# Sorting tokens by pair of experts: from marks at the end to lists in DRAM, written sequence by sequence

## The chip, the cores and the metric

The kernel runs on one core of a Trainium2 chip. The metric is the device time of one execution in microseconds (us); lower is better. Times are medians over runs; the profile is of one execution, taken by the hardware profiler. Engines are named as in the profile: PE (TensorE matmul), PEld (TensorE weight load), DVE (VectorE), ACT (ScalarE), POOL (GpSimd), SP (SyncE, which issues most DMAs). A name with a q, as SPq, is that engine's queue.

## The reference

One transformer block on 16 sequences of 512 tokens, 256 wide, in fp32. A layernorm feeds two branches, and both are added to the input:

```python
xn = layernorm(x)
q, k, v = xn @ Wq + bq, xn @ Wk + bk, xn @ Wv + bv      # 16 heads of 16
q, k = elu(q) + 1, elu(k) + 1
kv = einsum('bkhd,bkhm->bhdm', k, v)                    # linear attention
out = einsum('bqhd,bhdm->bqhm', q, kv) / max(einsum('bqhd,bkhd->bqh', q, k), eps)
attention = out @ Wo + bo
shared = swiglu(xn @ w_in.T) @ w_out.T
h = swiglu(xn @ w1.T)                                   # 512 wide, one for all experts
routed = sum(h * w_se[:, e] @ w2[e].T for e in range(8))
result = x + attention + shared + routed
```

The routing `w_se` picks for each token one of two groups of four experts, and the best two experts of that group. So a token belongs to one of 12 pairs of experts (6 to a group).

## The kernel before

There are 8192 tokens, in 64 tiles of 128 (`TT`; four to a sequence, `NT`). The work has two stages. In the first, a loop over the 16 sequences `b` computes attention, the shared branch and `h`, routes each token, and writes for each token a row of 770 numbers to DRAM (`h_d`): `h`, everything but the routed part, and the two weights of its pair. In the second, the tokens are taken sorted by pair, in tiles of 128 of one pair, at least 67 (`SURE`) and at most 75 (`TILES`). For each tile the rows are gathered with an indirect DMA (`Tiles.rows`, L943), turned (`turn`, L964 to L976), multiplied with the two experts' weights (`sums`, L993), weighted and added (L1000, L1003), and scattered to the output rows (L1006). To know which token stands where, the second stage needs two tables of [128 rows, 75 tiles]: `source` (the token to read) and `goal` (the row to write; too large for a place that stays empty, so that nothing is written). Making these two tables is what the change is about.

In iteration `b` of the loop come: the front of sequence b+1 (`residual` on POOL, L390; `project`, L412 to L430; `route`), `summarize` (L689), the normalization of b+2, the rows of `h` (`hidden_rows`, 14 products of 512 columns, L595), the key sum of b+1 (`key_sum`: two adds on POOL, L676 and L677, one product with ones, L679, and a copy `ksb` on DVE, L681), `attend` for b+1, the shared branch (`hidden`, L621), the small products with Wv and Wo (`values`, L708; `mix`, L731), and the outputs (`outputs`, L768; the add L777). The first sequence has plainer forms of the two branches (`first_rows`, L644 and L651; `first_hidden`, L663 and L669; weights are differenced beside them, L527). For the last sequence alone, the products with Wv and Wo are called from inside `hidden`.

`route` leaves in `hot` (bf16, [128, 64, 12]) a one at each token's pair, and POOL adds up in `ahead_of` (L515) how many tokens of each pair the earlier tiles had in the same partition.

The order on each engine comes from a scheduler that works at build time, except where the code fixes it: `keep_in_program_order` pins steps to the written order, `high_priority` moves steps ahead, `issue_after` holds one behind another. [...] Buffers come from pools that rotate: `ps_mm` has six PSUM banks, `ps_y` two, `work` two of each tag. A tile that takes a buffer waits for the last reader of the tile that had it. The key sums and the outputs take `ps_y` (the outputs of sequence 14 take `ps_mm`).

The sorting is `order()` (L806 to L924), a generator: each `yield` gives control back, and the loop calls `next` at chosen places, in part through `between`. Its steps: counts of each pair by two fp32 products (L813, L815); starts of the pairs, rounded up to whole tiles (L829); the slot of each of the 8192 tokens (L833 to L847); and the marks. A mark turns the slots round: for each of eight groups of eight tiles, DVE writes which of 128 rows (L877) and which of 75 tiles (L882) a token goes to, multiplied by the token's number (L886, L890), and PE adds `lo` times `hi` over all 64 tiles into one PSUM tile `pi` (L894, 64 bf16 products of 150 columns). From `pi` come `source` and `goal` (L908 to L923). These steps lie in the last two iterations: counts and slots in iteration 14, the marks between the outputs of 14 and the products of `hidden_rows` of 15.

Of the kernel before, what the change touches and what calls it, by code (L numbers as in the profile page):

```python
# [10 lines left out]
FP = mybir.dt.float32  # L11
AF = mybir.ActivationFunctionType
ALU = mybir.AluOpType
# [8 lines left out]
def block_kernel(  # L22
# [55 lines left out]
    TG = 8  # L78
    TR = 5
    assert TT % TG == 0  # L80
# [10 lines left out]

    h_d = dram.tile([TT * P, ROW], FP, name="h_d")

# [101 lines left out]
    def load_expert(i):  # L195
# [21 lines left out]
    before = const.tile([P, P], FP)  # L217
    nc.gpsimd.affine_select(
        out=before, in_=ones, pattern=[[1, P]],
# [4 lines left out]
    for j in range(EG):  # L224
        nc.gpsimd.memset(place[:, :, j : j + 1], float(j))
    BF = mybir.dt.bfloat16
    count = const.tile([P, P], BF)
    nc.gpsimd.iota(count, pattern=[[1, P]], base=0, channel_multiplier=0,
                   allow_small_or_imprecise_dtypes=True)
    number = const.tile([P, TT], BF)  # L230
    nc.gpsimd.iota(number, pattern=[[1, TT]], base=1, channel_multiplier=0,
                   allow_small_or_imprecise_dtypes=True)
    row = const.tile([P, 1], FP)
    nc.gpsimd.iota(row, pattern=[[0, 1]], base=0, channel_multiplier=1,
# [282 lines left out]
    def between(b, n):  # L517

        if b + 2 >= B:
            for _ in range(n or 0):  # L520
                next(steps_of_order)
# [68 lines left out]
    def hidden_rows(b, xs7, then):  # L590

        rows = {}

        def product(to, u, i, start, stop):
            tc.keep_in_program_order(nc.tensor.matmul(  # L595
                to, lhsT=xs7[i][:, ts(u, P)], rhs=w1_in[W7[i]], start=start, stop=stop,
                skip_group_check=True,
            ))

        def room(u, half):  # L600
            rows[u, half] = work.tile([P, HID], FP, tag="hr", name=f"hr_{b}_{u}_{half}", bufs=4)
            return rows[u, half]

        def done(u, half, silu, product):
            nc.sync.dma_start(out=h_d[ts(b * NT + 2 * half + u, P), 0:HID], in_=rows[u, half])

        seven(f"phr_{b}", product, lambda a: a, room, done, lambda n: between(b, then(n)))
# [89 lines left out]
    def small_sums(b, shape, name):  # L697

        if b + 1 == B:
            return ps_y.tile(shape, FP, tag="py", name=f"{name}_{b}"), tc.keep_in_program_order  # L700
        return ps_mm.tile(shape, FP, tag="mm", name=f"{name}_{b}"), lambda step: step
# [25 lines left out]
    def mix(b, vk):  # L727

        pm, pin = small_sums(b, [P, KD, D], "pm")
        for c in range(KD):  # L730
            pin(nc.tensor.matmul(  # L731
                pm[:, c, :], lhsT=vk[:, c, :], rhs=wo_sb[:, c, :], start=True, stop=True
            ))
        kvo = one.tile([P, KD, D], FP, tag="kvo", name=f"kvo_{b}")
        with tc.high_priority() if b + 1 == B else nullcontext():
            nc.scalar.copy(kvo, pm)
        return kvo
# [21 lines left out]
    def outputs(b, t, qT, kvo, hs):  # L759
# [6 lines left out]
        parts += [(qT[:, c, ts(t, P)], kvo[:, c, :]) for c in range(KD)]  # L766
        for i, (a, w) in enumerate(parts):
            nc.tensor.matmul(po, lhsT=a, rhs=w, start=(i == 0), stop=(i == len(parts) - 1))  # L768
        return po

    def gather(b, res, qT, kvo, hs, placed, then):

        for t in range(NT):
# [5 lines left out]
            between(b, then(t))  # L779
# [26 lines left out]
    def order():  # L806

        I32, U32 = mybir.dt.int32, mybir.dt.uint32
        total = keep.tile([P, NP], FP)
        nc.vector.tensor_copy(total, ahead_of[:, TT, :])  # L810
        pc = ps_mm.tile([P, 2 * NP], FP, tag="mm", name="pc")
        tc.keep_in_program_order(
            nc.tensor.matmul(pc[:, 0:NP], lhsT=before, rhs=total, start=True, stop=True)  # L813
        )
        nc.tensor.matmul(pc[:, NP:], lhsT=ones, rhs=total, start=True, stop=True)  # L815
        pcs = keep.tile([P, 2 * NP], FP)
# [3 lines left out]
        nc.vector.tensor_scalar(ci, pcs[:, NP:], float(P - 1), None, ALU.add)  # L820
# [5 lines left out]
        nc.vector.tensor_copy(runs[0][:, PAD:], ci)  # L826
        for i, d in enumerate((1, 2, 4, 8)):
            a, r = runs[i % 2], runs[(i + 1) % 2]
            nc.vector.tensor_tensor(r[:, PAD:], a[:, PAD:], a[:, PAD - d : PAD - d + NP], ALU.add)  # L829
        starts = runs[0][:, PAD - 1 : PAD - 1 + NP]  # L830

        off = keep.tile([P, NP], FP)
        nc.vector.tensor_tensor(off, pcs[:, 0:NP], starts, ALU.add)  # L833
        sl = one.tile([P, TT, NP], FP, tag="low", name="sl")
        nc.vector.tensor_tensor(
            sl, ahead_of[:, 0:TT, :], off.unsqueeze(1).to_broadcast([P, TT, NP]), ALU.add
        )
        nc.vector.tensor_tensor(sl, sl, hot, ALU.mult)
        slot = keep.tile([P, TT], I32)
        slf = keep.tile([P, TT], FP)  # L840
        nc.vector.tensor_reduce(slf, sl, AX.X, ALU.add)
        nc.vector.tensor_copy(slot, slf)
        part = keep.tile([P, 2, TT], I32)
        nc.vector.tensor_scalar(part[:, 0, :], slot, P - 1, None, ALU.bitwise_and)
        nc.vector.tensor_scalar(part[:, 1, :], slot, 7, None, ALU.arith_shift_right)
        place_of = keep.tile([P, 2, TT], BF)
        nc.vector.tensor_copy(place_of, part)  # L847
# [12 lines left out]
        nc.vector.tensor_copy(where, of)  # L860
        yield


        pi = ps_y.tile([P, 2 * TILES], FP, tag="py", name="pi")

        los = x_all.rearrange("p b t d -> p (b t d)").bitcast(BF).rearrange("p (n t j) -> p n t j", t=TG, j=P)
        his = [
            a[:, B % 2].rearrange("p t d -> p (t d)").bitcast(BF)[:, 0 : TG * 2 * TILES].rearrange(
                "p (t i n) -> p t i n", t=TG, i=2
            )  # L870
            for a in (qq_all, kk_all, xn_all)
        ]

        def marks(g):
            row_of, tile_of = (place_of[:, i, ts(g, TG)].unsqueeze(2) for i in range(2))
            lo, hi = los[:, g % 4], his[g % 3]
            nc.vector.tensor_tensor(  # L877
                lo, count.unsqueeze(1).to_broadcast([P, TG, P]), row_of.to_broadcast([P, TG, P]),
                ALU.is_equal,
            )  # L880
            at_tile = one.tile([P, TG, TILES], BF, tag="at_tile", name=f"at_tile_{g}")
            nc.vector.tensor_tensor(  # L882
                at_tile, count[:, 0:TILES].unsqueeze(1).to_broadcast([P, TG, TILES]),
                tile_of.to_broadcast([P, TG, TILES]), ALU.is_equal,
            )
            nc.vector.tensor_tensor(  # L886
                hi[:, :, 0, :], at_tile,
                number[:, ts(g, TG)].unsqueeze(2).to_broadcast([P, TG, TILES]), ALU.mult,
            )
            nc.vector.tensor_scalar(hi[:, :, 1, :], at_tile, row, None, ALU.mult)  # L890

        def add(g):
            for t in range(TG):
                tc.keep_in_program_order(nc.tensor.matmul(  # L894
                    pi, lhsT=los[:, g % 4, t, :], rhs=his[g % 3][:, t].rearrange("p i n -> p (i n)"),
                    start=(g + t == 0), stop=(g * TG + t == TT - 1),
                ))


        for g in range(TT // TG + 2):  # L900
            if g > 1:
                add(g - 2)
                yield
            if g < TT // TG:
                marks(g)
                yield
        pis = keep.tile([P, 2, TILES], FP)
        nc.vector.tensor_copy(pis.rearrange("p i n -> p (i n)"), pi)  # L908
        free = keep.tile([P, TILES], FP)
        nc.vector.tensor_scalar(free, pis[:, 0, :], 0.0, float(2 * TT * P), ALU.is_equal, ALU.mult)  # L910
        tok = keep.tile([P, TILES], FP)
        nc.vector.scalar_tensor_tensor(
            tok, pis[:, 0, :], float(P), pis[:, 1, :], ALU.mult, ALU.add
        )
# [6 lines left out]
        nc.vector.tensor_scalar(source, tok, float(-P), 0.0, ALU.add, ALU.max)  # L921
        goal = keep.tile([P, TILES], U32)
        nc.vector.scalar_tensor_tensor(goal, tok, float(-P), free, ALU.add, ALU.add)  # L923
# [109 lines left out]
    xs[2] = load_x(2)  # L1033
    for b in range(B):
# [4 lines left out]
        if b + 2 == B:  # L1039
# [4 lines left out]
            steps_of_order = order()  # L1044
        if b + 1 == B:
            sums7 = token_sums(b, xnT)
            hidden_rows(b, sums7, {2: 2, 6: 2, 9: 2, 13: 2}.get)
# [3 lines left out]
            *lists, filled = next(steps_of_order)  # L1051
# [9 lines left out]
        if b == 0:  # L1061
            first_rows(xnT)
        elif b + 1 < B:
            sums7 = token_sums(b, xnT)
            hidden_rows(b, sums7, {9: 1}.get)
# [5 lines left out]
        if b + 2 == B:  # L1071
            next(steps_of_order)
# [3 lines left out]
        if b + 1 < B:  # L1076
# [13 lines left out]
        if b + 2 == B:  # L1090
            next(steps_of_order)
# [5 lines left out]
        else:  # L1097
            gather(b, res, qT, kvo, hs, normed[b + 2][2]() if b + 2 < B else None, {0: 2, 1: 2, 3: 2}.get)
# [66 lines left out]
```

## Time and profile before

| | us |
|---|---|
| median of 3 runs (1039.69 to 1040.49) | 1040.03 |
| the profiled execution | 1033.23 |
| its span, first to last instruction | 1031.5 |
| PE busy | 1004.9 |
| DVE busy | 779.4 |
| ACT busy | 488.1 |
| POOL busy | 254.8 |

A row of the time line gives start, length, engine, line, operation, `output<-input` with the sizes, and how many instructions it holds; at its end in brackets the idle time of the engine before it and what ended that. A row of the waits says who waited for whom: time in all, number of times, longest. PE ran at full clock (1.00 in each stretch looked at). The fp32 products are recorded as two matmuls each. One sequence of the middle takes about 47 us (the first `project` product of the sequence at 644.7 and of the next at 692.07); the second stage begins at 789.84 us.

### The profile page before, as it was taken

How to read it: one execution, taken by the hardware profiler on the slowest of the kernel's cores; microseconds unless marked ns; L12 is line 12 of the kernel's file. 1: busy time of each engine (PE TensorE's matmuls, PEld its weight loads, DVE VectorE, ACT ScalarE, POOL GpSimd, SP SyncE). 2: the span in 40 equal slices, each digit the busy share in tenths (PEclk: the TensorE clock that was granted, in tenths of full speed). 3: DMA queues.
4: the chain of work that ended last, by engine and by line, in shares of the span. 5: the costliest groups of instructions: out<-in, count | busy, mean ns of one | idle time of the engine just before them, and what ended most of it. 6: DMA issues, size and time to landing. Idle time of an engine off the chain costs nothing. (4 is left out here: it accounts for less than half of the span.)

```text
span 1031.5 us, 12407 instructions
## 1 busy us (share of the span) xinstructions
PE 1004.9 (97%) x3704; PEld 681.7 (66%) x3704; DVE 779.4 (76%) x1974; ACT 488.1 (47%) x893; POOL 254.8 (25%) x359
## 2 busy tenths in 40 slices
PE   7999999999999999999999999999899999999996
PEld 5466868677786868686777768686667344444442
DVE  5978687878778787878787877868975776666663
ACT  3525353535445253535343534425136576766671
POOL 5302020111202021110202020201012766555652
PEclk9999999999999999999999999999999999999999
DMA  7063534525152522314141313221235755555440
GB/s 220 16 177 107 141 104 101 147 59 154 51 163 54 161 84 81 122 42 143 37 128 56 110 55 123 72 77 61 62 110 146 225 172 153 147 156 157 150 147 30
DMA packets 130339, 116.08 MB, mean 113 GB/s; under 512 B 72637, under 2 KB 114109, under 8 KB 130272
## 3 DMA queue, kind: packets, MB, share of 16 engines
q1 hardware_dynamic: 120064, 77.43, 25.7%
q0 software_dynamic: 9392, 37.58, 12.2%
q8 instruction: 31, 0.51, 0.2%
q10 hardware_dynamic: 816, 0.27, 0.2%
q14 instruction: 36, 0.29, 0.1%
HBM read 65.36 MB, written 50.27 MB: 112 GB/s over the span
## 5 line engine op out<-in xcount | busy, mean ns | idle before, releaser
L993 PE MATMUL py<-w_sb,hT 128*128 x536 | 230.7, 592 | 1.7 <-DVE hT L976 1.6
L993 PEld LDWEIGHTS py<-w_sb,hT 128*128 128x128 f32 x536 | 101.7, 190 | 130.1 <-issue 129.1
L768 PE MATMUL po<-wout_sb,hs_all 128*128 128x256 f32 x480 | 116.6, 380 | 1.4 <-DVE hs_all L580 1.4
L390 POOL TENSOR_TENSOR res<-x_all,bo_sb 128x256 f32<-128x256 f32 x64 | 48.5, 792 | 274.4 <-DMA h_d<-res 203.4
L768 PEld LDWEIGHTS po<-wout_sb,hs_all 128*128 128x128 f32 x480 | 89.2, 190 | 15.1 <-DVE hs_all L580 3.4
L1006 POOL DMA_INDIRECT out<-y,goal x67 | 67.8, 1012 | 76.3 <-DVE y L1003 65.3
L676 POOL TENSOR_TENSOR k<-kk_all 128x512 f32<-128x512 f32 x16 | 20.9, 1307 | 258.3 <-DVE sm L458 247.7
L777 DVE TENSOR_TENSOR res<-po,res 128x256 f32<-128x256 f32 x60 | 25.4, 424 | 76.6 <-PE po L768 76.5
L398 ACT ACTIVATE km<-km 128x1024 f32<-128x1024 f32 x16 | 16.9, 1057 | 138.7 <-DVE km L397 134.4
L595 PE MATMUL phr_w<-w_sb,ss 128*128 128x512 f32 x120 | 61.5, 594 | 2.2 <-DVE ss L538 1.9
L768 PE MATMUL po<-kvo,qT 128*128 128x256 f32 x240 | 61.7, 383 | 0.0
L621 PE MATMUL phs_w<-ss,win_sb 128*128 128x256 f32 x240 | 61.6, 379 | 0.0
L621 PE MATMUL phs_t<-xnT,win_sb 128*128 128x256 f32 x240 | 61.6, 379 | 0.0
L595 PE MATMUL phr_t<-w_sb,xnT 128*128 128x512 f32 x120 | 61.3, 593 | 0.0
L595 PE MATMUL phr_t<-w_sb,ss 128*128 128x512 f32 x120 | 59.4, 597 | 0.0
L621 PE MATMUL phs_t<-ss,win_sb 128*128 128x256 f32 x240 | 59.1, 379 | 0.0
L689 PE MATMUL pxk<-kk_all,xn_all 128*128 128x256 f32 x256 | 58.0, 379 | 0.0
L412 PE MATMUL pk<-wkr_sb,xnT 128*128 128x266 f32 x240 | 57.2, 387 | 0.0
L423 PE MATMUL pq<-w_sb,xnT 128*128 128x256 f32 x240 | 54.2, 379 | 0.0
L689 PEld LDWEIGHTS pxk<-kk_all,xn_all 128*128 128x128 f32 x256 | 48.5, 190 | 6.7 <-issue 0.2
L964 ACT COPY hb<-qq_all 32x256 f32<-32x256 f32 x108 | 43.4, 402 | 17.1 <-DMA qq_all<-h_d,source 9.7
L412 PEld LDWEIGHTS pk<-wkr_sb,xnT 128*128 128x128 f32 x240 | 45.4, 190 | 8.0
(216 smaller groups left out, 1966.0 us busy)
## 6 DMA issues: line engine op xcount, KB each, us to landing
h_d<-hr SPq DMA_DIRECT2D x64, 256.0 KB, 2.5
q_d<-qq_all SPq DMA_DIRECT2D x16, 512.0 KB, 2.8
qb<-q_d SPq DMA_DIRECT2D x64, 128.0 KB, 3.1
w_sb<-in_w SPq DMA_DIRECT2D x64, 128.0 KB, 3.5
h_d<-res SPq DMA_DIRECT2D x60, 129.0 KB, 1.9
x_all<-in_x SPq DMA_DIRECT2D x15, 512.0 KB, 4.8
xn_d<-xn_all SPq DMA_DIRECT2D x14, 512.0 KB, 3.9
xb<-xn_d SPq DMA_DIRECT2D x56, 128.0 KB, 2.8
```

The source lines that it names most:

```text
L390: nc.gpsimd.tensor_tensor(res[:, t, 0:D], xt[:, t, :], bo_sb, ALU.add)
L412: nc.tensor.matmul(pk, lhsT=xnT[:, k, ts(t, P)], rhs=wkr_sb[:, k, :], start=(k == 0), stop=(k == KD - 1),)
L423: nc.tensor.matmul(pq[:, t, :], lhsT=xnT[:, k, ts(t2 + t, P)], rhs=wq_sb[:, k, :], start=(k == 0), stop=(k == KD - 1),)
L595: tc.keep_in_program_order(nc.tensor.matmul(to, lhsT=xs7[i][:, ts(u, P)], rhs=w1_in[W7[i]], start=start, stop=stop, skip_group_check=True,))
L621: tc.keep_in_program_order(nc.tensor.matmul(split(to)[:, f, :], lhsT=win_in[W7[i]][:, ts(2 * u + f, P)], rhs=xs7[i], start=start and f == ...
L676: nc.gpsimd.tensor_tensor(k2, kk[:, 0:2, :], kk[:, 2:4, :], ALU.add)
L689: nc.tensor.matmul(pxk[:, c, :], lhsT=xn[:, t, ts(c, P)], rhs=kk[:, t, :], start=(t == 0), stop=(t == NT - 1),)
L768: nc.tensor.matmul(po, lhsT=a, rhs=w, start=(i == 0), stop=(i == len(parts) - 1))
L777: nc.vector.tensor_tensor(res[:, t, 0:D], po, res[:, t, 0:D], ALU.add)
L964: nc.scalar.copy(there[ts(q, Q), a - near, 0:n, :], self.hg[ts(a, Q), 0:n, ts(q, W)])
L993: nc.tensor.matmul(py.rearrange("p j d -> p (j d)"), lhsT=self.hT[:, f, ts(j, P)], rhs=w2_sb[:, f, bass.ds(regs[i % TR], 2 * D)], start=(f ...
L1006: stored = nc.gpsimd.indirect_dma_start(out=out_rows, out_offset=bass.IndirectOffsetOnAxis(ap=self.goal[:, i : i + 1], axis=0), in_=y, in_ ...
```

## The change

The marks go away. In their place each pair has a list in DRAM, `lists_d`, with room for all tokens (8192 entries of 8 words), cleared at the start to a number too large for a token. As each sequence is routed, `enlist(b)` finds for each of its tokens the rank within its pair with two bf16 products: the tokens of the same tile in earlier partitions (`before`), and all tokens of earlier tiles (ones times `ahead_of`). Four DVE steps make an address of it, and four indirect DMAs on POOL write the tokens' numbers into the lists. At the end, `order` needs the counts and starts alone; one indirect gather fetches, for each of the 75 tiles, its 128 entries, DVE copies the token numbers out, PE turns them, and `source` and `goal` are read from the result. `order` now runs in iteration 14 between `hidden` and the outputs, its last part behind the outputs. Sequence 14 takes the form of the last one for the products with Wv and Wo (inside `hidden`, in `ps_y`), and its outputs add the attention part first. `before` becomes bf16, and the `row` constant counts in steps of 128.

```diff
@@ constants
-    before = const.tile([P, P], FP)
+    ones_bf = const.tile([P, P], BF)
+    nc.gpsimd.memset(ones_bf, 1.0)
+    before = const.tile([P, P], BF)
...
+    lists_d = dram.tile([NP * TT + TILES - TT + 1, P * WORDS], U32, name="lists_d")
...
+    ids = const.tile([P, TT], U32)
+    nc.gpsimd.iota(ids, pattern=[[P, TT]], base=0, channel_multiplier=1)
+    lists_at = const.tile([P, NP], FP)
+    nc.gpsimd.iota(lists_at, pattern=[[LIST, NP]], base=0, channel_multiplier=0,
...
@@ new functions; between() is gone
+    def clear_lists():
+        free = work.tile([P, P * WORDS], U32, tag="blocks", name="free")
+        nc.gpsimd.memset(free, FREE)
+        R = lists_d.shape[0]
+        for r in range(0, R, P):
+            n = min(P, R - r)
+            nc.sync.dma_start(out=lists_d[r : r + n, :], in_=free[0:n, :])
+
+    def enlist(b):
+        pr = ps_y.tile([P, NT, NP], FP, tag="py", name=f"pr_{b}")
+        flat = pr.rearrange("p t c -> p (t c)")
+        mine = hot[:, ts(b, NT), :]
+        nc.tensor.matmul(flat, lhsT=before, rhs=mine.rearrange("p t c -> p (t c)"), start=True, stop=False)
+        nc.tensor.matmul(
+            flat, lhsT=ones_bf, rhs=ahead_of[:, ts(b, NT), :].rearrange("p t c -> p (t c)"),
+            start=False, stop=True,
+        )
+        rk = small.tile([P, NT, NP], FP, tag="rk", name=f"rk_{b}")
+        nc.vector.tensor_tensor(rk, pr, lists_at.unsqueeze(1).to_broadcast([P, NT, NP]), ALU.add)
+        nc.vector.tensor_tensor(rk, rk, mine, ALU.mult)
+        rf = small.tile([P, NT], FP, tag="rf", name=f"rf_{b}")
+        nc.vector.tensor_reduce(rf, rk, AX.X, ALU.add)
+        spot = small.tile([P, NT], U32, tag="spot", name=f"spot_{b}")
+        nc.vector.tensor_scalar(spot, rf, float(WORDS), None, ALU.mult)
+        for t in range(NT):
+            put = nc.gpsimd.indirect_dma_start(
+                out=entries,
+                out_offset=bass.IndirectOffsetOnAxis(ap=spot[:, t : t + 1], axis=0),
+                in_=ids[:, b * NT + t : b * NT + t + 1], in_offset=None,
+            )
...
@@ small_sums, mix
-        if b + 1 == B:
+        if b + 2 >= B:
...
@@ outputs
+        if b + 2 == B:
+            parts = parts[KH:] + parts[:KH]
@@ order
-        pc = ps_mm.tile([P, 2 * NP], FP, tag="mm", name="pc")
...
-        nc.tensor.matmul(pc[:, NP:], lhsT=ones, rhs=total, start=True, stop=True)
+        pc = ps_y.tile([P, NP], FP, tag="py", name="pc")
+        nc.tensor.matmul(pc, lhsT=ones_bf, rhs=ahead_of[:, TT, :], start=True, stop=True)
...
+        jump = keep.tile([P, NP], FP)
+        nc.vector.tensor_scalar(jump, runs[0][:, PAD:], -1.0, float(LIST), ALU.mult, ALU.add)
...
-        off = keep.tile([P, NP], FP)
...
-            marks(g)
...
+        past = keep.tile([P, NP - 1], FP)
+        nc.vector.tensor_scalar(past, starts[:, 1:], row, None, ALU.is_le)
+        nc.vector.tensor_tensor(past, past, jump[:, 0 : NP - 1], ALU.mult)
+        begin = keep.tile([P, 1], FP)
+        nc.vector.tensor_reduce(begin, past, AX.X, ALU.add)
+        part = keep.tile([P, 1], U32)
+        nc.vector.tensor_scalar(part, begin, row, 1.0 / P, ALU.add, ALU.mult)
+        got = work.tile([P, P * WORDS], U32, tag="blocks", name="got")
+        nc.gpsimd.indirect_dma_start(
+            out=got[0:TILES, :], out_offset=None, in_=lists_d,
+            in_offset=bass.IndirectOffsetOnAxis(ap=part[0:TILES, :], axis=0),
+        )
+        tokens = keep.tile([P, P], FP)
+        nc.vector.tensor_copy(
+            tokens[0:TILES, :], got[0:TILES, :].rearrange("p (n w) -> p n w", w=WORDS)[:, :, 0]
+        )
         yield
+        pi = ps_y.tile([P, TILES], FP, tag="py", name="pi")
+        nc.tensor.transpose(pi, tokens[0:TILES, :], ident[0:TILES, 0:TILES])
...
+        nc.vector.tensor_scalar(source, pi, float(TT * P - 1), None, ALU.min)
...
+        nc.vector.tensor_copy(goal, pi)
@@ main loop
     xs[2] = load_x(2)
+    clear_lists()
...
-            hidden_rows(b, sums7, {2: 2, 6: 2, 9: 2, 13: 2}.get)
+            hidden_rows(b, sums7)
...
             sums = key_sum(b + 1, fronts[b + 1][2])
             queries[b + 1] = attend(b + 1, fronts[b + 1][1], sums)
+        if b == 0:
+            enlist(0)
+        if b + 1 < B:
+            enlist(b + 1)
...
-        if b + 1 < B:
+        if b + 2 < B:
             hs, made = hidden(b, sums7) if b else first_hidden(xnT)
             kvo = mix(b, values(b, xk, ksb))
...
-            gather(b, res, qT, kvo, hs, normed[b + 2][2]() if b + 2 < B else None, {0: 2, 1: 2, 3: 2}.get)
+            if b + 2 == B:
+                steps_of_order = order()
+                next(steps_of_order)
+            gather(b, res, qT, kvo, hs, normed[b + 2][2]() if b + 2 < B else None)
+            if b + 2 == B:
+                *lists, filled = next(steps_of_order)
```

## The prediction

> **What bounds the kernel now.** The page comes first: the span and the engines' shares.
>
> ```profile
> span 1031.5 us, 12407 instructions
> ...
> PE 1004.9 (97%) x3704; PEld 681.7 (66%) x3704; DVE 779.4 (76%) x1974; ACT 488.1 (47%) x893; POOL 254.8 (25%) x359
> ```
>
> TensorE (PE) is busy for all but 26.6 us. The list of its own waits says where the rest is:
>
> ```profile
> PE pt L335 <- DVE xn_all L328: 7.5, 5, 5.3
> PE pm L731 <- DVE rz L748: 2.5, 1, 2.5
> PE phr_w L595 <- DVE ss L538: 1.9, 1, 1.9
> PE py L993 <- DVE hT L976: 1.6, 1, 1.6
> PE phs L663 <- DVE hr L651: 1.5, 1, 1.5
> ...
> PE phr_w L595 <- DVE hr L574: 0.3, 1, 0.3
> PE pi L894 <- DVE qq_all L890: 0.2, 1, 0.2
> ```
>
> Start-up apart, PE stops once in the first sequence (L663), four times around the sorting (L731, L894, L538, L574) and once in the last stage. Elsewhere its rows follow each other without a gap. So what PE gains or loses between 20 and 800 us goes to the end in full. The time line of PE shows the sorting at work:
>
> ```profile
> 727.61 1.05 PE L708 MATMUL pvk<-xk,wv_sb 128*128 128x128 f32 x8
> 731.13 1.10 PE L731 MATMUL pm<-wo_sb,vk 128*128 128x256 f32 x4 [2.47 <-DVE rz L748]
> ...
> 743.98 0.70 PE L894 MATMUL pi<-xn_all,x_all 128*128 128x150 bf16 x8
> 744.52 1.06 PE L595 MATMUL phr_t<-w_sb,xnT 128*128 128x512 f32 x2
> 747.49 1.10 PE L595 MATMUL phr_w<-w_sb,ss 128*128 128x512 f32 x2 [1.91 <-DVE ss L538]
> ```
>
> A row's length includes a tail; the cost of a group is the distance to the next start: eight products of marks take 0.54 us (743.98 to 744.52). Last, the first sequence: PE, then VectorE (DVE).
>
> ```profile
> 48.66 1.02 PE L663 MATMUL phs<-xnT,win_sb 128*128 128x512 f32 x2
> 51.22 1.98 PE L663 MATMUL phs<-xnT,win_sb 128*128 128x512 f32 x4 [1.54 <-DVE hr L651]
> ```
>
> ```profile
> 53.48 0.68 DVE L527 TENSOR_TENSOR w_sb<-w_sb 128x512 f32<-128x512 f32 x1
> 54.08 0.42 DVE L681 COPY ksb<-pks 128x256 f32<-128x256 f32 x1
> 54.53 1.23 DVE L743 TENSOR_TENSOR qk<-qq_all,ksb 128x1024 f32<-128x1024 f32 x1
> ```
>
> Here DVE, not PE, is full: its rows have no idle time from 37.9 to 65.5 us.
>
> **Removed, on PE's path.** Eight groups of marks: 8 x 0.535 = 4.28 us, and 0.04 us after each, by which the next fp32 product starts later than its like (0.90 against 0.86 us): 0.32. The two fp32 count products (L813, L815): 711.15 to 711.51 and 0.09 after, 0.45. The stalls 2.47, 0.23, 1.91 and 0.33: 4.94. All four come from DVE, which works through the counts and marks (8 x (1.22 + 0.77 + 0.77 + 0.37) = 25 us) from 716 to 765 us. Sum 9.99. A check: from 692.07 to 779.48 PE took 87.41 us; the same products at the distances of an undisturbed sequence come to 76.75, so 10.7 is there. I take 10.3. The stalls do go: in the changed kernel as built, the products with Wv and Wo of sequence 14 lie inside its `hidden` (as those of 15 did), and the token sums (L538 to L541) stand right behind the last products of `hidden`.
>
> **Added: the ranks.** Each `enlist` is two bf16 products of 48 columns, standing right behind the key sum on PE. No row has that form; the nearest is the marks' bf16 pair of load and product, 67 ns (0.535/8), so 0.13 us for two and 0.04 for the return to fp32. Against the change speaks a rule of the Trainium skill ("TensorE: Matmul & The Clock Gate", section "LDWEIGHTS (loading the stationary operand)"): a load costs about its columns divided by 1.2 in ns, 107 for 128, however few columns the product has. The trace has 98 ns for one such load, but hides part of it. By the row, 14 x 0.17 = 2.4 us; by the rule, 14 x (0.21 + 0.04) = 3.6. I take 0.20 each, nearer to the row: 2.8 us for sequences 2 to 15. Their inputs are in time: `ahead_of` was done at 661.1, the key sum came at 667.2. The four DVE steps of each (0.17 to 0.20 by rows like L829 and L858, some 0.7 us) fall where DVE waits some 1.4 us in each sequence for ACT and PE (L574 13.5 us in 28 waits, L579 6.8 in 14); without that cover they would cost up to 0.7 x 14 = 10 us.
>
> **Added: a longer stall in the first sequence.** `enlist(0)` and `enlist(1)` both come there. The `ps_y` pool has two buffers: the key sum of 1 takes one, the ranks of 0 the other, the ranks of 1 the first again. So they wait for the copy `ksb` (L681) of that key sum, and in the changed kernel PE has them behind the first pair of `phs` products, with the other twelve behind. The copy ends at 54.50, and no new step stands ahead of it on the full DVE. PE gets 0.2 us of ranks and a first fp32 load done and goes on at about 54.9 instead of 51.22: +3.7 us, the ranks of 0 and 1 included. Nothing gives this back: `phs` then ends at 65.3, DVE (8 more steps, 1.2 us) has `hs` at 66.1 and `vk` at 67.6, and PE comes to `pm` at 68.0. Bounds: 3.3 (ranks free) to 5.
>
> **Moved: the list.** `order` now starts behind `hidden(14)`. Call T the moment PE takes the count product (about 0.1 us). PE then has 24 products of `outputs` (48 records x 0.216 = 10.4 us) and reaches the transpose `pi` at T + 10.5; all of `hidden_rows(15)` is queued behind it. The chain to it: DVE finishes `hs` first (in sequence 13 the slot behind L580 was 1.4 us after the like of T), then L584 0.6, four token sums 1.4, one add of `res` 0.35 and 17 small steps at some 0.15: T + 6.4. POOL's gather: the one at 795.13 was read at 799.43, 4.3 us. The copy of the tokens 0.25. So `pi` is ready near T + 11.2 and PE stands 0.7 us; bounds 0 and 2.5. The transpose costs some 0.25 with its return (0.18 for L335's). Count product and transpose: 0.35. The tokens' copy keeps only the last add of `res`, `source` and `goal` waiting on DVE, and the next user, the first gather of rows, comes a dozen us later.
>
> **Added, off the path.** The 64 scatters on POOL: 1.01 us each by L1006, 0.3 between. In a sequence they start when DVE has `spot`, some 8 us after the key sum (about 675 in sequence 13's time), and end at 680; POOL's next work is this:
>
> ```profile
> 659.88 1.22 POOL L515 TENSOR_TENSOR ahead_of<-ahead_of,hot 128x12 bf16<-128x12 bf16 x4 [3.79 <-DVE hot L498]
> 694.88 3.23 POOL L390 TENSOR_TENSOR res<-x_all,bo_sb 128x256 f32<-128x256 f32 x4 [33.78 <-DMA h_d<-res]
> ```
>
> It waits until 694.9 anyway; a scatter would have to take 5 us to be felt. They write words of 4 bytes, and the skill ("DMA: Bandwidth & Descriptors", section "Specifications") says that below 512 bytes a DMA reads, changes and writes back. The row has 3.0 us to landing for scatters of 1 KB rows; the last put of 15 then lands near T + 2. Doubled by the rule, T + 5, still ahead of the gather at T + 6.5. By either the sum is the same. The clearing (6 DMAs of 512 KB and a rest) has SP from 20.5 to 42.0, when the queue was empty; at 2.8 us each, as `q_d` writes of that size landed, it ends by 38. Twice that delays writes at 42 and 50 whose data is needed at 64 or later. POOL's fill of 128x1024 (some 1.7 us, eight times the 0.21 of 128x128) lies in its idle time from 9.4 to 13.9.
>
> **Sum.** -10.3 + 2.8 + 3.7 + 0.35 + 0.7 = -2.75 us on the profiled span of 1031.5, whose execution took 1033.23. The runs' median is 1040.03, 6.8 above; I carry the difference over: 1037.3, a ratio of 0.9974. A change of under 0.2% (2.1 us) can hardly be told from none here, so this stands just past that line.
>
> **The rivals.** (a) *As summed*, 1037.3, its own range 1035.8 to 1038.8: chance 0.50. (b) *The first sequence's stall is hidden*: DVE is full there for reasons of its own, and if PE's delay were made good while it fills `hs`, 3.3 us return: 1034.0. Against it: PE has no gap behind 65. 0.10. (c) *The list comes late*: the gather waits for data written by 64 scatters, and the chain has no slack; 2.5 us of stall instead of 0.7: 1039.1, no change. For it: gathers landed in 3.7 to 9.9 us. 0.20. (d) *The stalls come back*: DVE's small chain sits in the same place as the old one, between L584 and the token sums; if half of the 4.94 returns as other waits and the ranks cost the rule's price, -2.75 + 2.5 + 0.8 = +0.5: 1040.6. 0.08. (e) *POOL becomes late*, on the other side: each scatter holds POOL past the moment when `res` and with it the next sequence's key sum and `ahead_of`, which are queued behind, are due, and PE waits at the ranks in every sequence. It decides from 5 us a scatter on; 0.5 us of wait in 14 sequences is +7: 1044. Against it: 1.0 us by the row. 0.12, which also stands for what I do not see.
>
> **How the numbers follow.** Faster by over 0.2% (below 1037.95): three quarters of (a), all of (b), a part of (c): 0.52. Slower (above 1042.1): (e) and a little of (d): 0.14. Same: 0.34. The range takes in (a), (b), (c) and (d) and leaves out (e) and an end of (b): 1034.0 to 1041.6.
>
> **What would show it.** Right: PE's wait in the first sequence is about 5 us and names `ksb`; no waits named `rz` or `ss` near 731 and 747; the pair of ranks takes 0.15 to 0.25 us on PE's time line; a wait of `pi` for the tokens of 0 to 2.5 us; scatters near 1 us that end 10 us ahead of `res`. Wrong: a wait of the ranks for POOL in every sequence, DVE behind in the middle sequences, or a stall of PE in the first sequence that is made good before 100 us.

## The result: 3.8 us slower

The changed kernel takes 1043.86 us (median of 7 runs, 1042.78 to 1044.73) against 1040.03 us of the kernel before (7 runs, 1039.69 to 1040.76): a ratio of 1.0034, 95% interval 1.0025 to 1.0044. The forecast was 1037.3 us with a range from 1034.0 to 1041.6. Its profiled execution took 1044.26 us. The runs of this study were made on several chips; on one of them all profiles, of either kernel, have a stop of PE in the second stage, as the profile of the changed kernel here has and the first profile of the kernel before has not, and the times of both kernels are some 6 us longer on that chip.

The page of the changed kernel begins so:

```profile
span 1042.5 us, 12495 instructions
...
PE 1005.5 (96%) x3670; PEld 680.2 (65%) x3670; DVE 756.8 (73%) x2000; ACT 488.1 (47%) x893; POOL 330.3 (32%) x426
...
L554 POOL DMA_INDIRECT lists_d<-ids,spot x64 | 74.1, 1158 | 184.1 <-DVE spot L552 157.5
```

PE is as busy as before (1005.5 against 1004.9 us), though 64 of its products are gone: what it no longer does is made up by 32 short products and by products at half speed. POOL's new 75 us are the puts, 1.16 us each. PE's waits (waiting engine and line, what it waited for; total, times, longest):

```profile
PE pr L541 <- DVE ksb L721: 4.9, 1, 4.9
PE py L981 <- DVE hT L964: 4.7, 1, 4.7
...
PE pxk L729 <- DVE sm L465: 0.8, 1, 0.8
PE pi L902 <- DVE tokens L897: 0.3, 1, 0.3
```

The four stalls of the sorting (for `rz`, `ss`, `hr` and the marks) are gone, as forecast, and so is the 1.5 us for `hr` in the first sequence. In their place stand the forecast wait of the ranks for `ksb` and a short one of `pi`. The wait for `hT` is the stop in the second stage. The wait for `sm` stands in neither profile of the kernel before; the part on the prediction comes back to it. The first sequence on PE's time line:

```profile
49.20 1.02 PE L703 MATMUL phs<-xnT,win_sb 128*128 128x512 f32 x2
55.08 0.20 PE L541 MATMUL pr<-hot,before 128*128 128x48 bf16 x1 [4.85 <-DVE ksb L721]
55.10 0.21 PE L542 MATMUL pr<-ahead_of,ones_bf 128*128 128x48 bf16 x1
55.14 3.76 PE L703 MATMUL phs<-xnT,win_sb 128*128 128x512 f32 x4
58.69 1.91 PE L703 MATMUL phs<-xnT,w_sb 128*128 128x512 f32 x2
```

The products queued behind the ranks started only when these had run, at 55.14. Before, such a group of four products took 1.82 us from start to start (51.22 to 53.04) and one of two 0.86. Here they take 3.55 and 1.71. The busy times by stretch, with the granted clock as the number behind PE's, say why:

```profile
core 0: us, PE busy (x), PEclk, DMA share, GB/s
49.20:53.88 4.68, 1.02 (x3) 1.00 0.47 158
53.88:60.71 6.83, 5.63 (x9) 0.50 1.10 252
60.71:68.28 7.57, 7.57 (x18) 1.00 0.59 195
```

For 6.83 us the granted clock is a half. The first 1.2 us of that lie in the wait and cost nothing more; from the end of the wait to the first product with Wv PE takes 13.14 us (55.14 to 68.28), where before it took 10.41 (51.22 to 61.63), so the halved clock costs 2.7 us on top of the wait. The sorting:

```profile
722.94 0.19 PE L541 MATMUL pr<-hot,before 128*128 128x48 bf16 x1
...
722.99 1.11 PE L661 MATMUL phs_t<-xnT,win_sb 128*128 128x256 f32 x4
...
736.92 0.17 PE L851 MATMUL pc<-ahead_of,ones_bf 128*128 128x12 bf16 x1
736.95 1.11 PE L810 MATMUL po<-kvo,qT 128*128 128x256 f32 x4
...
747.81 0.29 PE L902 MATMUL pi<-ident,tokens 75*128 75x75 f32 x1 [0.26 <-DVE tokens L897]
747.94 1.07 PE L635 MATMUL phr_t<-w_sb,xnT 128*128 128x512 f32 x2
```

A pair of ranks costs 0.05 us and 0.09 in the product behind it; the count 0.03 + 0.08; the transpose 0.26 of wait, 0.13 and 0.04. All as forecast or less.

**Where the time went.** Marks on PE's time line split the span (first product with Wv of a sequence, L708 and L748; start of the first and of the last product of the second stage, L993 and L981; end of the span). The last two columns compare profiles with the same second stage: the changed kernel above against the kernel before profiled again (first experiment), and the changed kernel profiled again (experiment with 65 and 79 writes) against the first profile of before.

| stretch | forecast | above | again |
|---|---|---|---|
| start to the first product with Wv | +3.7 | +7.2 | +6.9 |
| from there to that of sequence 13 | +2.6 (13 ranks of 0.20) | +1.3 | +1.3 |
| from there to the second stage: sorting | -9.05 (-10.3 + 0.2 + 0.35 + 0.7) | -10.8 | -10.4 |
| second stage, first to last product | 0 | -1.0 | -0.7 |
| last product to the end of the span | 0 | +7.1 | +7.1 |
| sum (of the spans, unrounded) | -2.75 | +3.7 | +4.2 |

At the start of the second stage the changed kernel is 2.3 us ahead (787.66 against 789.96), near the forecast for the whole. The loss lies where PE has nothing left to do: from its last product to the end the span has 17.0 us instead of 9.9. No group of the page names it: in that view these instructions do not count as busy. The view by line of the statements that close the program has them (minimum, median and maximum in ns, start of the first and last). Before:

```profile
L1121 POOLq INC_SWDGE_SEM  x1: 1007/1007/1007, 1026.2 to 1026.2; - x1
```

```profile
L1161 POOLq DRAIN  x3: 51/103/3418, 1027.2 to 1031.2; - x3
```

After:

```profile
L1113 POOLq INC_SWDGE_SEM  x1: 2316/2316/2316, 1030.6 to 1030.6; - x1
```

```profile
L1153 POOLq DRAIN  x3: 51/103/8727, 1032.9 to 1042.2; - x3
L1153 DVEq EVENT_SEMAPHORE  x2: 21/21/21, 1041.8 to 1042.4; - x2
```

Behind the last scatter of `out` POOL does a semaphore step and then a drain: 1.01 + 3.42 us before, 2.32 + 8.73 after. The other engines' last semaphore instructions (here DVE's, which had drained at 1028.0) come when this drain is over, at 1041.8. That is 6.6 us of the 7.1; the semaphore step itself starts 0.5 us later behind the last product (5.1 us instead of 4.6). Before had 140 indirect DMAs in its program, the changed kernel has 205.

### The profile page after: what moved, and what is told of

It is laid out like the page before. It is cut to its first block, busy times and chain, and to the rows that moved or that the text cites. A ratio compares the mean times of both kernels' runs of the same rounds, so it can differ in the third digit from the quotient of the medians.

```text
span 1042.5 us, 12495 instructions
## 1 busy us (share of the span) xinstructions
PE 1005.5 (96%) x3670; PEld 680.2 (65%) x3670; DVE 756.8 (73%) x2000; ACT 488.1 (47%) x893; POOL 330.3 (32%) x426
## 3 DMA queue, kind: packets, MB, share of 16 engines
q1 hardware_dynamic: 120952, 80.62, 26.6%
## 4 chain that ended last, share of the span: by engine, by line
PE 86%; DVE 7%; DMA 2%; issue 1%; another core or an unknown queue 1%; SPq 1%; ACT 0%; DVEq 0%; POOL 0%; ACTq 0%; POOLq 0%
PE py L981 21%; PE po L810 13%; PE phr_t L635 10%; PE phs_t L661 9%; PE pxk L729 5%; PE pk L419 5%; PE phr_w L635 5%; PE pq L430 5%; PE phs_w L661 4%; PE phr_l L635 2%; PE phs_l L661 2%; PE pm L771 1%; PE phs L703 1%; PE pvk L748 1%; PE po L829 1%
## 5 line engine op out<-in xcount | busy, mean ns | idle before, releaser
L981 PE MATMUL py<-w_sb,hT 128*128 x536 | 232.4, 596 | 6.1 <-DVE hT L964 4.7
L981 PEld LDWEIGHTS py<-w_sb,hT 128*128 128x128 f32 x536 | 102.3, 191 | 135.6 <-issue 133.4
L554 POOL DMA_INDIRECT lists_d<-ids,spot x64 | 74.1, 1158 | 184.1 <-DVE spot L552 157.5
L405 ACT ACTIVATE km<-km 128x1024 f32<-128x1024 f32 x16 | 16.9, 1058 | 139.3 <-DVE km L404 135.0
L952 ACT COPY hb<-qq_all 32x256 f32<-32x256 f32 x108 | 43.4, 402 | 18.5 <-DMA qq_all<-h_d,source 10.4
```

Of the source, the lines that this page charges most:

```text
L554: put = nc.gpsimd.indirect_dma_start(out=entries, out_offset=bass.IndirectOffsetOnAxis(ap=spot[:, t : t + 1], axis=0), in_=ids[:, b * NT + ...
L952: nc.scalar.copy(there[ts(q, Q), a - near, 0:n, :], self.hg[ts(a, Q), 0:n, ts(q, W)])
L981: nc.tensor.matmul(py.rearrange("p j d -> p (j d)"), lhsT=self.hT[:, f, ts(j, P)], rhs=w2_sb[:, f, bass.ds(regs[i % TR], 2 * D)], start=(f ...
```

## Experiments

In each, the time is given with the ratio to the kernel before on the same chip.

**The kernel before, profiled again.** No edit.

> The kernel before, unchanged, profiled once more, because its first profiled execution (1033.23 us) lies 6.8 us under the median of its runs. Theory A, a local event: in its usual execution something that the first profile doesn't have costs about 6.8 us in one or two places, for instance an end that takes longer after the last product (9.3 us there, 16.4 us in the changed kernel) or a stop of PE in the second stage with a half-speed clock after it (as at 817 to 825 us in the changed kernel). Then this profile has a span near 1038.5 us and shows the place. Theory B, an execution like the first: span 1031.5 us, end 9.3 us, no place to show.

1040.07 us, ratio 0.9998 (0.999 to 1.0007); span 1038.7. Theory A. The end is as in the first profile (1.01 + 3.42 us, 9.9 us from the last product). PE's waits have a new row against the first profile, the same as in the changed kernel:

```profile
PE py L993 <- DVE hT L976: 4.6, 1, 4.6
```

Behind it the clock is halved for 6.83 us, and the second stage takes 238.9 us instead of 231.8. So the 6.8 us that I carried from the profiled execution to the median are this stop (7.1 us between the two profiles). It is on both sides of the comparison and explains nothing of the result; the end does.

**The second ranks later.** `enlist(1)` behind the outputs of sequence 0. (An interval of a sequence is, here and below, the one that ends with its first product with Wv.)

```diff
-        if b + 1 < B:
+        elif b + 1 < B:
             enlist(b + 1)
...
             gather(b, res, qT, kvo, hs, ...)
+            if b == 0:
+                enlist(1)
```

> The changed kernel, with the ranks of sequence 1 moved behind the outputs of sequence 0. Theory A: the wait of 4.85 us for ksb in the first sequence costs twice, itself (about 3.4 us net) and a half-speed clock behind it for 6.8 us (3.4 us lost), so without it the run is 6.5 us shorter: 1037.4 us, no half-speed stretch near 54 to 61 us. Rival: the clock falls there whatever stands in front, and only the wait is saved: 1040.4 us.

1040.47 us, ratio 1.0001 (0.9992 to 1.001): 3.4 us less than the changed kernel, in number the rival's. The trace shows another sum. There is no half-speed stretch in the first sequence, and its first product with Wv comes at 63.18 instead of 68.28, 5.1 us earlier (6.2 without the difference at the start, where PE waited 1.9 us for `sm` here and 0.8 there), near theory A's 6.5. Sequence 1 then takes 49.0 us instead of 47.4, 1.6 us of it given back: DVE has the four steps of these ranks there, and PE waits for it, in one place 0.8 us, the rest in smaller pieces.

```profile
PE phr_w L635 <- DVE hr L614: 0.8, 1, 0.8
```

So wait and clock together are most of the loss of the first sequence, and this place for the ranks was a poor one.

**The lists added to the kernel before.** `clear_lists`, `enlist` and their constants, called where the changed kernel calls them; nothing reads the lists, the marks stay.

```diff
+    clear_lists()
...
+        if b == 0:
+            enlist(0)
+        if b + 1 < B:
+            enlist(b + 1)
```

> The kernel before, with clearing, ranks and the 64 puts added in the same places as in the changed kernel, the lists left unread; the marks stay. Theory A, the costs simply add: 16 pairs of ranks at 0.15 us = 2.4, first sequence +6.5 - 0.3, and the end of the program longer by 6.6 us because POOL has 64 more indirect DMAs to account for (0.1 us each): 1040.0 + 15.2 = 1055 us, and the time from PE's last product to the end is 16 us. Rival: the end does not depend on their number: 1048.6 us, end 9.3 us.

1055.32 us, ratio 1.0132 (1.0109 to 1.0154): 15.2 us more, the sum of theory A. The end is as forecast (+7.0 us in the traces, against the kernel before profiled again); of the other parts the first sequence lost more than forecast (8.8 us, not 6.2) and the sorting and the second stage less than nothing (-0.9 and -0.8), so that the sum is so exact is luck. 204 indirect DMAs, semaphore step 2.30 us, drain 8.65, 16.9 us from the last product to the end. PE waits 4.9 us for `ksb` in the first sequence, and the clock is halved for 6.83 us at 55.5.

**Each put twice.**

```diff
             put = nc.gpsimd.indirect_dma_start(out=entries, ...)
+            again = nc.gpsimd.indirect_dma_start(out=more, ...)
```

> The changed kernel, each put issued a second time into a second list that nothing reads. Theory A: the end of the program grows with the number of indirect DMAs that POOL has issued (0.1 us each): from PE's last product to the end 16.4 + 6.6 = 23 us, time 1043.9 + 6.6 = 1050.5 us. Rival: the long end belongs to single executions and not to their number: end 9 to 17 us, time 1043.9 us, since the 1.3 us more of POOL per put lie in its idle time.

1054.18 us, ratio 1.0155 (1.0105 to 1.0204), and neither theory. The end became shorter, 12.0 us, with 269 indirect DMAs:

```profile
L1162 POOLq DRAIN  x3: 51/103/5215, 1043.2 to 1049.0; - x3
```

The time is lost elsewhere: sequences 1 to 7 take between 48.0 and 52.8 us instead of 47.4 to 47.6, so puts of twice the number are no longer free there; what holds PE in these places stays open. And the end does not simply grow with the number. It could be periodic: if 65 more cost 5.31 us of drain (0.0817 us each), 269 has the drain of 162, and 107 make a turn.

**Fourteen more puts.** 219 indirect DMAs:

```diff
+            if 40 <= b * NT + t < 54:
+                again = nc.gpsimd.indirect_dma_start(out=more, ...)
```

> The changed kernel, with 14 further puts (a second time for the columns of tokens 40 to 53, into a list that nothing reads), so POOL issues 219 indirect DMAs instead of 205. The ends seen so far: 140 DMAs 1.01 + 3.42 us (semaphore step and drain of POOL), 204: 2.30 + 8.64, 205: 2.32 + 8.73, 269: 1.45 + 5.21. Theory A, the end counts the DMAs since the last of a period of about 107 (0.082 us each in the drain, 0.020 in the step): 219 lies behind a turn, drain 1.1 us and step 0.5 us, some 9.4 us less than before the edit, time 1034.5 us. Theory B, it grows with the number and 269 was short for another reason: drain 9.9 us, step 2.6, time 1045.3 us.

1028.03 us, ratio 0.9945 (0.9928 to 0.9961). This chip has no stop in the second stage (before is at 1033.85 us), so the forecast is to be read as a difference: 9.4 us less. The changed kernel, put on a like chip later, is 4.3 us over before; this one is 5.8 us under it: 10.1 us less, by adding 14 DMAs. In the traces of the two, 9.3 us of that lie behind the last product (7.7 us instead of 17.05).

```profile
L1123 POOLq INC_SWDGE_SEM  x1: 480/480/480, 1023.7 to 1023.7; - x1
```

```profile
L1163 POOLq DRAIN  x3: 51/103/1207, 1024.2 to 1026.0; - x3
```

The turn was forecast before the run, with 1.1 us for the drain. All ends of the study, whatever the kernel:

| indirect DMAs | profiles | semaphore step, us | drain, us |
|---|---|---|---|
| 140 | 2 | 1.01 | 3.42 |
| 199 | 1 | 2.20 | 8.24 |
| 204 | 1 | 2.30 | 8.65 |
| 205 | 5 | 2.31 to 2.32 | 8.73 |
| 219 | 4 | 0.48 | 1.21 |
| 269 | 1 | 1.45 | 5.22 |

From 140 to 199 and on to 205 the drain grows by 0.082 us for each DMA, from 219 to 269 by 0.080, and somewhere between 205 and 219 it falls back. It makes no difference whether a DMA moves 128 words (140 against 205, in the kernel before) or 128 rows of 3 KB (199 against 205): 0.082 us each.

**65 writes in the kernel before.** First with nothing to hold them back, then behind the counts of sequences 2 to 14, and there with 79 as well (six where the diff has five; `last` is the last add of `ahead_of`):

```diff
+        for i in itertools.islice(puts, 5 if b > 1 else 0):
+            with tc.issue_after(last.ins):
+                nc.gpsimd.indirect_dma_start(out=more_d, ...)
```

> The kernel before, with 65 indirect writes of 128 words to a list that nothing reads, four in each sequence where POOL is idle, and nothing else of the change: 205 indirect DMAs. Theory A, the end alone: drain 8.7 and step 2.3 us, 6.6 to 7.1 us more than before, time 1047 us, PE's time line as before up to its last product. Rival: the writes cost in the sequences too (POOL, or the DMA queues), more than 2 us on top, 1049 us or more; or the end stays at 4.4 us and the time at 1040.

> The kernel before, with 65 unread indirect writes of 128 words, five behind the counts of each of sequences 2 to 14, in POOL's idle time. Theory A, only the end pays for them: semaphore step 2.3 us and drain 8.7, 6.6 us more than before, no other difference over 0.5 us. Rival: POOL's time or the queues cost too: more than 8 us.

> The same with 79 writes: 219 indirect DMAs. Theory A, the end is a count that has turned: drain 1.2 us and a short semaphore step, so 3 us less than the kernel before, and 9.7 us less than with 65 writes, with 14 writes more. Rival, it grows with the number: 8 us more than before.

1076.98 us (ratio 1.0411, 1.0387 to 1.0436), 1055.50 us (1.0216, 1.0199 to 1.0233) and 1053.44 us (1.0216, 1.018 to 1.0251). As measurements of the end alone in time they failed. The first had all its writes set at the start of the program, ahead of POOL's adds for the key sum (PE waits for those 17.8 us). In the second, sequences 9 to 13 take 49.8 to 50.4 us instead of 47.8, with PE waiting for `hs_all`, and in the third 50.3 to 51.4:

```profile
PE po L781 <- DVE hs_all L593: 11.9, 10, 1.5
```

The order that the scheduler gave DVE is another one there; I did not follow this up. The end itself can be read in all three: 2.31 + 8.73 us with 65 writes, twice, and 0.48 + 1.21 with 79, as in the changed kernel with the same numbers. So the end follows the number of indirect DMAs, not the change.

**The changed kernel again, on the chip of the last two.** No edit.

> The changed kernel unchanged, for one chip with the other three: its distance from the kernel before with 65 writes (same number of indirect DMAs, so the same end) is then the change without its end. By the traces so far the start of the second stage came 2.3 us earlier with the change; that should be the distance, 2.3 us (1.8 to 3). If the end were not the missing term, the distance would be that of the two kernels themselves, -3.8 us.

1037.71 us, ratio 1.0042 (1.0025 to 1.0059), span 1035.7. The comparison that I meant fails with the 65 writes. The trace gives its own answer: second stage at 787.66 us, 2.2 us ahead of the first profile of before (forecast 2.3), and 17.05 us from the last product to the end.

**Without the second gather.** The first three pairs of tiles are not gathered again at the start of the second stage, so the outputs of the last sequence are missing in them.

```diff
-    for w in tiles[: AHEAD - 1]:
-        w.rows()
...
-        if g == 0:
-            tiles[AHEAD - 1].rows()
```

> The changed kernel, without the second gather of the first three pairs of tiles (their rows keep the base as it was at the first gather, so these tiles lack the outputs of the last sequence). It leaves out 6 of 73 gathers, those at 793 to 805 us. Asked is the stop of PE in the second stage near 817 us, which all profiles but the first of the kernel before have (4.6 us, and a half-speed clock behind it). Theory A, the gathers crowd there and something comes late: without them no stop, second stage 231.5 us long instead of 237.9. Rival: it has nothing to do with them, 237.9 us. The end of the program changes too, with 199 indirect DMAs: drain 8.2, step 2.2 us.

1035.26 us, ratio 1.0014 (1.0004 to 1.0023). The run fell on a chip without the stop, so it says nothing on it; the second stage took 229.6 us, against 231.0 and 231.8. Its end, 2.20 + 8.24 us, is as forecast. What makes the stop stays open.

**Own buffer for the second ranks.** As with fourteen more puts, and:

```diff
+        if b == 1:
+            pr = ps_mm.tile([P, NT, NP], FP, tag="mm", name=f"pr_{b}")
```

> As the run with 14 further puts, and the ranks of sequence 1 in a buffer of the other pool, so that PE does not wait for ksb. If that wait and the half-speed clock behind it are what the first sequence lost: 5 to 6.5 us less than the run with 14 further puts alone, 1028.5 us where that one has 1034.5. Rival: the ranks of 1 then wait for something else that comes as late, the routing of sequence 1 or a buffer: no gain.

1024.66 us, ratio 0.9911 (0.9895 to 0.9928): 3.4 us less than with the puts alone, less than the 5 to 6.5 forecast. PE no longer waits for `ksb`; but `phs` lacks the bank and waits for its reader:

```profile
46.99 1.99 PE L716 MATMUL phs<-xnT,win_sb 128*128 128x512 f32 x4 [0.28 <-ACT sa_hr L702]
51.70 2.03 PE L716 MATMUL phs<-xnT,w_sb 128*128 128x512 f32 x2 [2.73 <-DVE hr L704]
```

```profile
51.70:55.20 3.50, 3.50 (x4) 0.51 1.03 344
```

(Busy time of PE, the granted clock, DMA share, GB/s.) A wait of 2.73 us was enough for the clock to be halved again, for 3.41 us.

**Second ranks with the third.** As the last, and the ranks of sequence 1 taken in iteration 1, ahead of those of 2:

```diff
-        if b == 0:
-            enlist(0)
+        if b == 1:
+            enlist(1)
         if b + 1 < B:
-            enlist(b + 1)
+            enlist(b + 1 if b else 0)
```

> The changed kernel with 14 further puts and the ranks of sequence 1 taken in the next sequence, ahead of those of 2, with a buffer of the larger pool. If the first sequence loses its time to the second ranks alone (the wait, the clock, and four steps on DVE): 2 to 3 us less than the run that only gave them a buffer (ratio 0.9911 there), 0.9885. Rival: it only moves the loss into sequence 1: 0.9911 or more.

1023.08 us, ratio 0.9902 (0.9886 to 0.9919), 10.4 us under the kernel before. The interval overlaps with the last one's, so the step between the two stands on the traces: the second stage begins at 782.36 instead of 784.55 us. PE waits in the first sequence as the kernel before does, 1.5 us for `hr`, and the clock stays whole:

```profile
52.28:62.68 10.40, 10.40 (x24) 1.00 1.04 263
```

Sequence 1 takes 47.9 instead of 47.4 us. Against the first profile of before, 7.5 us are gained up to the second stage, 0.3 in it and 2.4 at the end. The last part is not the change's: the kernel before, with 79 writes, had the same short end.

## Why the prediction was wrong

The step that failed stands under "What bounds the kernel now": "The list of its own waits says where the rest is." Of the 26.6 us in which PE is not busy, the waits account for 17.1 (15.5 in the rows shown there, 1.6 in two that were left out). The other 9.3 us lie behind PE's last product, where it waits for nothing more and the program still runs:

```profile
994.57 27.63 PE L993 MATMUL py<-w_sb,hT 128*128 x64
```

This row ends at 1022.2, the span at 1031.5. The sum let that end stand as it was, and "Added, off the path" asked of the 64 scatters only when POOL and the queues would be free, and put them at nothing. The runs show in its place: from 140 to 205 each indirect DMA makes the end of the program 0.10 us longer (0.082 in the drain, 0.020 in the step before it), so the 65 of the change cost 6.6 us, and the end took 7.1 us more. The profile of before had the row (3.42 us of drain after 140 indirect DMAs); I didn't look past the last product. One profile could not have given the price of a DMA, nor that it turns back.

- *Removed, 10.3.* From the first `pk` product of sequence 15 to the start of the last outputs the changed kernel takes 77.31 us (699.99 to 777.30) against 87.41. With one pair of ranks (0.14), the count (0.11) and the transpose with its wait (0.43) taken off, 76.63 are left; so 10.8 went, and the check (10.7) was nearer than the sum.
- *Ranks, 0.20 each.* 0.14 us each by the rows; sequences 2 to 8 became longer by 0.13. The row's price (0.17) was the nearer and the rule's (0.25) too high. Over 13 sequences 1.3 us in place of 2.6.
- *First sequence, +3.7.* The wait was right in place, length (4.85 us for a forecast of about 5), cause and releaser; PE went on at 55.1 (forecast 54.9). Two terms were missing. One is the clock: of the +7.2 us, 6.4 lie behind the key sum's product of sequence 1 (45.76 against 44.97 in the kernel before profiled again), and that is the forecast and the 2.7 of the halved clock. In the profile again, with 3.41 us at half clock, the clock costs 1.6. The Trainium skill ("TensorE: Matmul & The Clock Gate", section "HAM oscillation — how this bites in real kernels") warns of PE-idle gaps over some 3.4 us. I read that page for the loads and not for this wait, which is such a gap; in a later run 2.73 us was enough, so the measurement decides here and not the 3.4.
- *The clearing, at nothing.* This is the other missing term of the first sequence: "Added, off the path" saw the clearing of the lists delay writes alone. SP issues it right behind the load of `x_all` for sequence 2. DVE had that load 4.75 us after its issue before (20.03 to 24.78) and 5.8 after (19.51 to 25.31); in all nine profiles with the clearing it took 5.4 to 6.5 us, in four without it 4.6 to 5.05 (the run with its writes at the start left aside). PE then waits for `sm` 0.4 to 2.1 us in the nine, and 0 to 1.1 in the four. That fits the +0.8 and +1.9 us ahead of the key sum's product; no run leaves out the clearing alone, so this cause is argued and not shown.
- *List, 0.7 of stall and 0.35.* 0.26 and 0.28. The gather left at T + 6.2 (forecast 6.4). The terms written there reach T + 10.95 and not 11.2 (6.4, 4.3 and 0.25), a stall of 0.45: 0.25 us of the 0.7 were a slip.
- *Scatters at 1.01 us, in POOL's idle time.* 1.16 us each and no wait of PE for POOL: right for 64, but for the end. Twice the number cost time in sequences 1 to 7, though that is 2.5 us a column of tokens and I had set the limit at 5. The page of the skill cited there for writes under 512 bytes gives no factor; the doubling was an estimate of mine, and no trace here has the landing of a put.
- *The difference of 6.8 us to the median, carried over.* Right, as the stop is in both kernels on such chips.

The other parts that were off nearly cancel, by luck: +3.2 to +3.5 in the first sequence, -1.3 at the ranks, -1.3 to -1.7 in the sorting, -0.7 to -1.0 in the second stage, which I had expected unchanged (why it is shorter stays open). Without the end the change gains 2.9 to 3.3 us, where 2.75 was forecast. None of the rivals had the right cause; (e) had the sign and 1044 us, for a wait that did not come.

## What to carry to other kernels

When a change adds indirect DMAs, look past the last product at the closing drain of POOL and see what it costs for the number that are there; hidden while they run is not free. A new wait of PE is to be costed with what the clock loses behind it: here waits up to 1.7 us left it whole, and every one of 2.7 us and more had it halved for at least 3.4 us, of which only the part behind the wait costs time (1.6 and 2.7 us in the changed kernel). And a small product that takes a buffer of a tight pool can hold up all that stands behind it; move it to an iteration where its reader is on time.

## What the runs showed of the hardware

- The closing drain of POOL depends on the number of indirect DMAs and turns back: 3.42 us at 140, 8.73 at 205, 1.21 at 219, 5.22 at 269. With the slope of 0.082 us, 219 has the drain of 113 and 269 that of 162, so the turn is at 106 to 107 DMAs; that it comes again at each further 106 or 107 was not measured. The Trainium skill ("DMA: Bandwidth & Descriptors", section "SWDGE vs HWDGE vs iDMA") says that POOL itself writes the descriptors of such DMAs into rings; that the turn is such a ring's is possible, and no run here shows it.
- Two of the chips ran the same kernels without the stop in the second stage: the kernel before took 1033.5 and 1033.9 us there, and 1040.1 on the third.
- Between 15 us and the last product of PE, all 15 waits of PE of 2.7 us and more in the profiles of this study have a stretch of half clock with them, 3.41 or 6.83 us long (up to 17.07 where PE waited 16 us). Of 15 waits from 1.8 to 2.5 us five have one, of 3.41 us: the wait of 2.5 us for `rz` in the kernel before has it in the second profile and not in the first. Waits up to 1.7 us have none.
